# Two-layer sequence model on one Trainium2 core: the second layer's TensorE instructions in a written order, with value matmuls by group and the last output split by heads

## The chip, the cores and the metric

The kernel runs on one core of one Trainium2 chip. The metric is device time in microseconds (us) of one execution. Everything is fp32. TensorE (PE) does all matrix products and all transposes, and writes to PSUM; VectorE (DVE), ScalarE (ACT) and GpSimd (POOL) do the rest; SyncE (SP) only issues transfers.

## The reference, cut to what matters

The input is 16 sequences of 256 tokens with 256 features. Both layers have the form x + s(xn) · silu(g(xn)), with xn the layer norm of x.

```
x  = L0_attn_x                               # [16, 256, 256]
xn = layernorm(x)
s  = linear recurrence(xn)                   # 32 complex states, scan over the 256 tokens
g  = silu(proj2(gelu(proj1(xn))))            # 256 -> 1024 -> 256
x  = x + s * g

xn = layernorm(x)
# s: latent attention, 16 heads, causal
q        = xn @ Wq                           # per head 128 'nope' + 64 'rope' features
kv       = xn @ Wkv_a                        # 64 latent + 64 rope features, one for all heads
c_kv     = rmsnorm(kv[:64]) * kv_norm_w
k_nope, v = split(c_kv @ Wkv_b)              # per head
scores   = (q_nope k_nope + rope(q_rope) rope(k_rope)) / sqrt(192), causal mask
s        = softmax(scores) @ v, all heads, @ Wo
# g: base linear + 2 of 8 low-rank experts, chosen by a router
g = silu(xn @ base_w.T + base_b + 2 * sum_e gate_e * (xn @ A_e) @ B_e)
x = x + s * g
```

## The kernel before, in words

The 4096 tokens are worked on in 8 chunks of 512 tokens (two sequences each); `X[ch]` stays in SBUF from beginning to end. Layer 0 runs over all chunks first, then layer 1.

**Layer 0** calls TensorE through a small wrapper, `pe = InOrder(nc.tensor)` (line 52 in the profile). It ties every TensorE instruction to the one before it, so that TensorE's program has them in the order in which the source calls them. Layer 0 also folds the key and value up-projections into the query and output weights (`wlat`, `wout`), so that attention in layer 1 works on the 64 latent features alone.

**Layer 1** calls `nc.tensor` itself. There the source order is a priority only, and a scheduler of the framework, working when the kernel is built, sets the order of each engine's instructions. The instructions of each engine then run in that fixed order, and wait for each other by semaphores.

The pieces of a chunk, with their lines:

- `norm_chunk`, `transpose_chunk` (`tp`, L160; copies into `xnT` L164 on ScalarE, L166 on VectorE),
- `kv_chunk` (`pkv`, L516): latent keys and values, the `row` tile, with a small chain over ScalarE, VectorE and GpSimd; `key_chunk` (`pk`, L546) transposes `row` into `kT`,
- `router_chunk` (`pm`, L560) with a long chain of small VectorE instructions for the two best experts, `mid_chunk` (`pmT`, L615), and `gate_part` 0 and 1 (`pg`, L628 and L632), after the second of which ScalarE applies Silu to the whole chunk (L635). Silu lies in another table of ScalarE than Exp, so that there is a table load before and one after it,
- `query_tile(ch, g, t)` (`pq`, L684): four tiles for a group `g` of four heads. Tiles 0 and 1 hold rope features; VectorE multiplies (L688), GpSimd adds (L700, L701) into `qrot`, and eight transfers on SP's queue bring the result into `qg`. Tiles 2 and 3 go to `qg` through ScalarE (L694),
- `finish_part(ch, j)` (`po`, L791): the output projection of 128 tokens, 8 matmuls over the pairs of heads, the product with the gate on VectorE (L796), the sum with `X` on GpSimd (L797), and a transfer to HBM issued by SP.

The attention is cut into **units**: a unit is one group of four heads of one sequence, so a chunk has 8 units and the kernel 64. The main loop has a step for each unit. In step `i` there are three `score_pack`s of unit `i` (`sc`, L726: mask L738 and maximum L740 on VectorE, Exp with its sum L745 on ScalarE, reciprocal L750 on VectorE, normalization of `pr` L753 on GpSimd), the three `turn_part`s of unit `i - 2` (`pt`, L765: four transposes into one PSUM bank and a copy into `pT` on ScalarE, L766), the `values` of the unit turned in the step before (`av`, L775, with a copy into `attT` L785), two query tiles of the next group, and at most two chunk pieces: one of the next chunk and one `finish_part` of the chunk before. In the source a step is:

```
for z in range(3):
    if u:
        score_pack(u, z)
    if v and z == 0:
        values(v)
    if w:
        turn_part(w, 2 - z)
    if z < 2:
        if nq:
            query_tile(nq[0], nq[1], nq[2] + z)
        if extra[z]:
            extra[z]()
```

PSUM has eight banks: pool `ps_m1` has four, which all the chunk pieces, `pq`, `av` and `po` take in turn; `ps_sc` has three, one for each pack of scores; `ps_pt` has one for the transposes. After the loop come the four `finish_part`s of the last chunk.

Of the kernel before, what the change touches and what calls it, by code (L numbers as in the profile page):

```python
# [18 lines left out]
P = 128  # L19
B, S, D = 16, 256, 256  # L20
NTOK = B * S
CH = 512
# [18 lines left out]
def tile_two_layers(ctx: ExitStack, tc: tile.TileContext, d: dict, out: bass.AP):  # L41
# [114 lines left out]
    def transpose_rows(psum, ptag, src, dst, tag, layer=0):  # L156
        for c in range(2):
            ps = psum.tile([P, CH], F32, tag=ptag, name=f"tp_{tag}_{c}")
            for j in range(TPC):
                (pe if layer == 0 else nc.tensor).transpose(  # L160
                    ps[:, j * P : (j + 1) * P], src[:, j, c * P : (c + 1) * P], ident
                )
# [319 lines left out]
    sm = ctx.enter_context(tc.tile_pool(name="sm1", bufs=3))  # L482
    x1 = ctx.enter_context(tc.tile_pool(name="x1", bufs=2))
    qm = ctx.enter_context(tc.tile_pool(name="qm1", bufs=3))
    qr = ctx.enter_context(tc.tile_pool(name="qr1", bufs=2))
# [19 lines left out]
    def transpose_chunk(ch):  # L505
        k = chunks[ch]
        k.xnT = x1.tile([P, 2, CH], F32, tag="xnT", name=f"xnT1_{ch}")
        transpose_rows(ps_m1, "m1", k.xn, k.xnT, f"1_{ch}", layer=1)

    def kv_chunk(ch):  # L510
# [3 lines left out]
        for j in range(TPC):  # L514
            for c in range(2):
                nc.tensor.matmul(  # L516
# [4 lines left out]
        sq = a2.tile([P, TPC, KVL], F32, tag="sq", name=f"sq_{ch}", bufs=1)  # L521
# [10 lines left out]
        ra = a2.tile([P, TPC, ROPE], F32, tag="ra", name=f"ra_{ch}", bufs=1)  # L532
        rb = a2.tile([P, TPC, ROPE], F32, tag="rb", name=f"rb_{ch}", bufs=1)
# [7 lines left out]
    def key_chunk(ch):  # L541
# [3 lines left out]
        for j in range(TPC):  # L545
            nc.tensor.transpose(pk[:, j * P : (j + 1) * P], row[:, j, :], ident)  # L546
# [3 lines left out]
    def router_chunk(ch):  # L550
# [3 lines left out]
        mid = a2.tile([P, TPC, P], F32, tag="mid", name=f"mid_{ch}", bufs=1)  # L554
        for jp in range(2):
            pm = ps_m1.tile([P, 2, 256], F32, tag="m1", name=f"pm_{ch}_{jp}")
            for j2 in range(2):
                j = 2 * jp + j2
                for c in range(2):
                    nc.tensor.matmul(  # L560
# [40 lines left out]
        mg = a2.tile([P, TPC, P], F32, tag="mg", name=f"mg_{ch}", bufs=1)  # L601
        for j in range(TPC):
            nc.vector.tensor_tensor(
                mg[:, j, :].rearrange("p (e r) -> p e r", r=LR),
# [3 lines left out]
        k.mg = mg  # L608

    def mid_chunk(ch):  # L610
# [3 lines left out]
        for j in range(TPC):  # L614
            nc.tensor.transpose(pmT[:, j * P : (j + 1) * P], mg[:, j, :], ident)  # L615
        k.mT = a2.tile([P, CH], F32, tag="mT", name=f"mT_{ch}")
        nc.vector.tensor_copy(k.mT, pmT)

    def gate_part(ch, jp):
# [5 lines left out]
        for j2 in range(2):  # L625
            cols = slice((2 * jp + j2) * P, (2 * jp + j2 + 1) * P)
            for c in range(2):
                nc.tensor.matmul(  # L628
# [3 lines left out]
            nc.tensor.matmul(pg[:, j2, :], k.mT[:, cols], wlb, start=False, stop=True)  # L632
# [26 lines left out]

    class Group:  # L660
# [4 lines left out]
    def query_tile(ch, g, t):  # L665
# [12 lines left out]
        for c in range(2):  # L678
# [5 lines left out]
            nc.tensor.matmul(ps, w, k.xnT[:, c, :], start=(c == 0), stop=(c == 1))  # L684
# [24 lines left out]
    class Unit:  # L709


        def __init__(self, i):
# [5 lines left out]
            self.nm = sm.tile([P, NQ], F32, tag="nm", name=f"nm_{self.n}")  # L718
            self.sr = sm.tile([P, NQ], F32, tag="sr", name=f"sr_{self.n}")

    def score_pack(u, pi):
        k, b, pack = chunks[u.ch], u.b, PACK[pi]
        qg = groups[u.ch, u.g].qg
        sc = ps_sc.tile([P, CH], F32, tag="sc", name=f"sc_{u.n}_{pi}")
        for a, o in pack:
            nc.tensor.matmul(  # L726
# [31 lines left out]
    def turn_part(u, z):  # L758
        if z == 2:
            u.pT = pp.tile([P, 12, P], F32, tag="pT", name=f"pT_{u.n}")  # L760
        pt = ps_pt.tile([P, CH], F32, tag="pt", name=f"pt_{u.n}_{z}")
        for y in range(4):
            a, kb = BLOCKS[4 * z + y]
            o = OFF[a] + kb * P
            nc.tensor.transpose(pt[:, y * P : (y + 1) * P], u.pr[:, o : o + P], ident)  # L765
        nc.scalar.copy(u.pT[:, 4 * z : 4 * z + 4, :], pt.rearrange("p (y f) -> p y f", y=4))  # L766

    def values(u):
        k, b = chunks[u.ch], u.b
        av = ps_m1.tile([P, 2, S], F32, tag="m1", name=f"av_{u.n}")  # L770
        for p2 in range(2):
            for kb in range(2):
                for hh in range(2):
                    hc = slice(32 * (2 * p2 + hh), 32 * (2 * p2 + hh) + 32)
                    nc.tensor.matmul(  # L775
# [7 lines left out]
        if b == 0:  # L783
            k.attT.append(a2.tile([P, 2, CH], F32, tag="attT", name=f"attT_{u.n}", bufs=6))
        nc.vector.tensor_copy(k.attT[u.g][:, :, b * S : (b + 1) * S], av)  # L785

    def finish_part(ch, j):
        k = chunks[ch]
        po = ps_m1.tile([P, CH], F32, tag="m1", name=f"po_{ch}_{j}")
        for p in range(NPAIR):  # L790
            nc.tensor.matmul(  # L791
                po[:, 0:D], k.attT[p // 2][:, p % 2, j * P : (j + 1) * P], wout[:, p, :],
                start=(p == 0), stop=(p == NPAIR - 1),
            )
        o = a2.tile([P, D], F32, tag="o", name=f"o_{ch}_{j}")
# [3 lines left out]
        nc.sync.dma_start(out_dram[t0 : t0 + P, :], o)  # L799

    for k in chunks:
        k.attT = []
    norm_chunk(0)
    transpose_chunk(0)
    for t in range(4):
        query_tile(0, 0, t)
    kv_chunk(0)
    router_chunk(0)
    key_chunk(0)
    mid_chunk(0)  # L810
    for jp in range(2):
        gate_part(0, jp)
# [3 lines left out]
    LAG = 2  # L816
    LAST = NCH * PER
    units = {}
    turned = None
    for i in range(LAST + LAG + 1):  # L820
# [116 lines left out]
```

## Time and profile before

| what | value |
|---|---|
| time, median of 3 runs | 1108.28 us (1103.82 to 1109.83) |
| profiled execution: time | 1110.37 us |
| profiled execution: span of the trace | 1107.9 us |
| mean granted TensorE clock | 0.991 |
| busy: PE, PEld | 1032.7 us (93%), 743.7 us (67%) |
| busy: DVE, ACT, POOL | 523.9, 506.3, 401.9 us (47%, 46%, 36%) |
| layer 1's first TensorE instruction | at 289.38 us |
| first score matmul | at 318.09 us |
| last score matmul | starts at 1069.8 us |

The page gives the busy time of each engine, its costliest groups of instructions by source line, and the chain that ended last. PE is the matmul part of TensorE and PEld its weight load; every fp32 matmul stands twice among the records, so that "x16" in the timeline are eight matmuls of the source. In the timeline a line is a run of equal instructions: start, length, engine, source line, tile written and tiles read, and in brackets the idle time of the engine just before it with what ended that. The ends of matmuls are modelled and overlap a little with the next start, so that the step from start to start is the better measure.

### The profile page before, as it was taken

What the parts mean: (1) busy time and instruction counts of PE and PEld (TensorE: products, weight loads), DVE (VectorE), ACT (ScalarE), POOL (GpSimd) and SP (SyncE); (2) the same over time, 40 slices, a digit from 0 to 9 for tenths busy, and PEclk for the clock granted to TensorE, in tenths of its full rate; (3) what the DMA queues carried; (4) which work ended last, traced back from release to release, by engine and by line L of the source; (5) the groups of instructions that cost most, each with busy time, mean ns of one, the idle gap of its engine ahead of it and who ended that gap; (6) DMA issues with size and microseconds to landing.
All of it is one profiled execution on the core that took longest, in us unless ns stands there. A gap on an engine that the chain in (4) does not pass through costs nothing.

```text
span 1107.9 us, 16585 instructions
## 1 busy us (share of the span) xinstructions
PE 1032.7 (93%) x5442; PEld 743.7 (67%) x5442; DVE 523.9 (47%) x1841; ACT 506.3 (46%) x1520; POOL 401.9 (36%) x718
## 2 busy tenths in 40 slices
PE   5899999999889989999999999899999989999987
PEld 2666677666666667776776677577667767776765
DVE  7731253221667555545544454464465445545331
ACT  2223222333245575454546445654555474455450
POOL 2243342222524434333344333343344334334431
PEclk9999999999989999999999999999999999999999
DMA  9430000000011121111111211111111211112110
GB/s 307 133 101 10 0 10 10 10 10 10 11 24 24 25 34 25 30 25 20 30 29 26 30 33 29 20 25 29 25 23 33 36 26 25 29 25 32 25 22 20
DMA packets 155462, 38.57 MB, mean 35 GB/s; under 512 B 137585, under 2 KB 153841, under 8 KB 155377
## 3 DMA queue, kind: packets, MB, share of 16 engines
q1 hardware_dynamic: 153680, 35.93, 15.9%
q10 hardware_dynamic: 1696, 1.58, 0.5%
q8 instruction: 44, 0.72, 0.3%
q14 instruction: 42, 0.34, 0.1%
HBM read 14.42 MB, written 4.19 MB: 17 GB/s over the span
## 4 chain that ended last, share of the span: by engine, by line
PE 80%; ACT 8%; DVE 6%; issue 3%; POOL 1%; DMA 1%; POOLq 0%; ACTq 0%; SPq 0%; DVEq 0%
PE pq L684 17%; PE sc L726 11%; PE pf L52 9%; PE po L791 9%; PE ph L52 9%; PE av L775 8%; PE pt L765 7%; ACT pr L745 3%; PE pg L628 3%; ACT qg L694 2%; ACT pT L766 2%; PE pg L632 1%; PE py L52 1%; PE pm L560 1%; PE pkv L516 1%
## 5 line engine op out<-in xcount | busy, mean ns | idle before, releaser
L753 POOL TENSOR_SCALAR pr<-pr,sr 128x256 f32<-128x256 f32 (+7 forms) x512 | 189.3, 389 | 291.5 <-DVE sr L750 220.9
L745 ACT ACTIVATE pr<-sc,nm 128x256 f32<-128x256 f32 (+7 forms) x512 | 189.0, 380 | 75.4 <-DVE nm L740 67.4
L766 ACT COPY pT<-pt 128x512 f32<-128x512 f32 x192 | 112.9, 588 | 240.6 <-PE pt L765 240.3
L726 PEld LDWEIGHTS sc<-kT,qg 128*128 128x128 f32 x1024 | 157.8, 191 | 37.5 <-issue 23.1
L726 PE MATMUL sc<-kT,qg 128*128 128x256 f32 (+7 forms) x1024 | 173.8, 303 | 3.7 <-ACT qg L694 2.9
L765 PE MATMUL pt<-ident,pr 128*128 128x128 f32 x768 | 123.8, 281 | 14.5 <-ACT pT L766 14.5
L740 DVE TENSOR_REDUCE nm<-sc 128x1 f32<-128x256 f32 (+7 forms) x512 | 127.8, 299 | 3.7
L775 PE MATMUL av<-pT,row 128*64 128x256 f32 (+1 forms) x1024 | 100.3, 338 | 27.2 <-ACT pT L766 27.2
L684 PE MATMUL pq<-xnT,wrope 128*128 128x512 f32 x256 | 121.6, 598 | 0.3 <-ACT xnT L164 0.3
L684 PE MATMUL pq<-xnT,wlat 128*128 128x512 f32 x256 | 120.7, 593 | 0.0
L791 PE MATMUL po<-wout,attT 128*128 128x256 f32 x512 | 115.9, 380 | 0.0
L791 PEld LDWEIGHTS po<-wout,attT 128*128 128x128 f32 x512 | 97.5, 191 | 25.0 <-issue 11.6
L52 PE MATMUL ph<-xnT,p1T 128*128 128x512 f32 x256 | 113.2, 600 | 0.0
L52 PE MATMUL pf<-p2T,hT 128*128 128x256 f32 x512 | 113.0, 379 | 0.0
L688 DVE TENSOR_TENSOR qmul<-pq,rot_q 128x512 f32<-128x512 f32 x128 | 84.1, 681 | 55.0 <-PE pq L684 55.0
L765 PEld LDWEIGHTS pt<-ident,pr 128*128 128x128 f32 x768 | 89.8, 147 | 29.0 <-issue 22.9
L775 PEld LDWEIGHTS av<-pT,row 128*64 128x64 f32 x1024 | 64.9, 139 | 62.4 <-ACT pT L766 40.8
L52 PEld LDWEIGHTS pf<-p2T,hT 128*128 128x128 f32 x512 | 96.7, 190 | 13.3 <-issue 0.5
L745 ACT ACTIVATION_READ_ACCUMULATOR pr<-sc,nm 128x1 f32 x512 | 103.9, 203 | 0.0
L52 PEld LDWEIGHTS ph<-xnT,p1T 128*128 128x128 f32 x256 | 49.1, 193 | 59.5 <-issue 58.1
L694 ACT ACTIVATE qg<-pq 64x512 f32<-64x512 f32 x128 | 75.8, 592 | 28.3 <-PE pq L684 26.4
L701 POOL TENSOR_TENSOR qrot<-qmul,qmul 128x512 f32<-128x512 f32 x32 | 40.7, 1273 | 88.2 <-DVE sr L750 53.9
(174 smaller groups left out, 1040.3 us busy)
## 6 DMA issues: line engine op xcount, KB each, us to landing
qg<-qrot SPq DMA_DIRECT2D x256, 64.0 KB, 2.2
out_dram<-o SPq DMA_DIRECT2D x32, 128.0 KB, 1.7
x<-in_x_dram SPq DMA_DIRECT2D x7, 512.0 KB, 8.7
wqn<-in_wq_nopeT_dram SPq DMA_DIRECT2D x4, 512.0 KB, 4.5
wo<-in_Wo_dram SPq DMA_DIRECT2D x4, 512.0 KB, 5.6
w<-v SPq DMA_DIRECT2D x16, 128.0 KB, 2.3
wraw<-in_wq_rope_dram SPq DMA_DIRECT2D x1, 1024.0 KB, 9.8
x<-in_x_dram SPq DMA_DIRECT2D x4, 128.0 KB, 3.4
```

Of the source, the lines that this page charges most:

```text
L52: r = getattr(self.engine, name)(*args, **kw)
L684: nc.tensor.matmul(ps, w, k.xnT[:, c, :], start=(c == 0), stop=(c == 1))
L688: nc.vector.tensor_tensor(q.mul[t][:, r, :].rearrange("p (b s) -> p b s", b=2), ps2, bc(rot_q[:, r, :], 2), ALU.mult,)
L694: nc.scalar.mul(q.qg[0:64, :, 2 * (t - 2) + hh, :], ps[64 * hh : 64 * hh + 64, :].rearrange("p (a q) -> p a q", q=32), SCALE,)
L726: nc.tensor.matmul(sc[:, o : o + 32 * (a + 1)], qg[:, b * NQ + a, :, :].rearrange("p h q -> p (h q)"), k.kT[:, b * S : b * S + 32 * (a + 1 ...
L740: nc.vector.tensor_reduce(u.nm[:, a : a + 1], sc[:, o : o + 32 * (a + 1)], AX.X, ALU.max, negate=True)
L745: nc.scalar.activation(u.pr[:, OFF[a] : OFF[a] + w], sc[:, o : o + w], AF.Exp, bias=u.nm[:, a : a + 1], accum_out=u.sr[:, a : a + 1],)
L753: nc.gpsimd.tensor_scalar(v, v, u.sr[:, a : a + 1], 1.0, ALU.mult, ALU.mult)
L765: nc.tensor.transpose(pt[:, y * P : (y + 1) * P], u.pr[:, o : o + P], ident)
L766: nc.scalar.copy(u.pT[:, 4 * z : 4 * z + 4, :], pt.rearrange("p (y f) -> p y f", y=4))
L775: nc.tensor.matmul(av[64 * hh : 64 * hh + 64, p2, P * kb : S].rearrange("p (a q) -> p a q", q=32), k.row[:, 2 * b + kb, 0:KVL], u.pT[:, 8: ...
L791: nc.tensor.matmul(po[:, 0:D], k.attT[p // 2][:, p % 2, j * P : (j + 1) * P], wout[:, p, :], start=(p == 0), stop=(p == NPAIR - 1),)
```

## The change

1. **Written order.** All TensorE calls of layer 1 go through `pe` as well, so that TensorE's program follows the source.
2. **Values by group.** `values` is called in odd steps only, for units `i - 5` and `i - 4` together, just after the first score pack. `pT` gets three buffers (two before).
3. **Chunk pieces dealt anew.** Silu's half `gate_part(ch, 1)` moves to step 1 of its own chunk, the router from step 3 to 5, `kv_chunk` from 2 to 3, key and mid together to step 6, `gate_part(ch + 1, 0)` to 7. `finish_part`s stay in steps 3 to 6. In even steps with one piece it goes into the second slot.
4. **Start.** `kv_chunk(0)` comes first after the transposes, the last two query tiles after the router and the keys; `mid_chunk(0)` and the gate halves move into steps 0 and 1 of the loop.
5. **End.** The last chunk's output is split by heads: the matmuls over the first 6 pairs of heads of all four row blocks run after the last transposes and before the last two `values`, in four PSUM banks (three of them from `ps_sc`), and those of the last 2 pairs after.
6. **Output transfers** are issued by GpSimd instead of SP.
7. **Buffers.** Small tiles 3 to 2, `qmul` 3 to 2, `qrot` 2 to 1, `mT` 2 to 1; `sq`, `ra`, `rb`, `mid` share one tile, and `mg` is written over `mid`.

```diff
-                nc.tensor.matmul(                      # and so in every piece of layer 1
+                pe.matmul(
...
-    sm = ctx.enter_context(tc.tile_pool(name="sm1", bufs=3))
+    sm = ctx.enter_context(tc.tile_pool(name="sm1", bufs=2))
...
-    qm = ctx.enter_context(tc.tile_pool(name="qm1", bufs=3))
-    qr = ctx.enter_context(tc.tile_pool(name="qr1", bufs=2))
+    qm = ctx.enter_context(tc.tile_pool(name="qm1", bufs=2))
+    qr = ctx.enter_context(tc.tile_pool(name="qr1", bufs=1))
...
-        sq = a2.tile([P, TPC, KVL], F32, tag="sq", name=f"sq_{ch}", bufs=1)
+        tmp = a2.tile([P, 3, TPC, KVL], F32, tag="tmp", name=f"tmp_{ch}", bufs=1)
+        sq, ra, rb = tmp[:, 0], tmp[:, 1], tmp[:, 2]
...
-            u.pT = pp.tile([P, 12, P], F32, tag="pT", name=f"pT_{u.n}")
+            u.pT = pp.tile([P, 12, P], F32, tag="pT", name=f"pT_{u.n}", bufs=3)
...
-    def finish_part(ch, j):
+    def finish_begin(ch, j, p0, p1):
         k = chunks[ch]
-        po = ps_m1.tile([P, CH], F32, tag="m1", name=f"po_{ch}_{j}")
-        for p in range(NPAIR):
-            nc.tensor.matmul(
-                po[:, 0:D], k.attT[p // 2][:, p % 2, j * P : (j + 1) * P], wout[:, p, :],
+        if p0 == 0:
+            pool, tag = (ps_sc, "sc") if ch == NCH - 1 and j < 3 else (ps_m1, "m1")
+            k.po[j] = pool.tile([P, CH], F32, tag=tag, name=f"po_{ch}_{j}")
+        for p in range(p0, p1):
+            pe.matmul(
+                k.po[j][:, 0:D], k.attT[p // 2][:, p % 2, j * P : (j + 1) * P], wout[:, p, :],
                 start=(p == 0), stop=(p == NPAIR - 1),
             )
+
+    def finish_part(ch, j, p0=0):
+        k = chunks[ch]
+        finish_begin(ch, j, p0, NPAIR)
+        po = k.po[j]
...
-        nc.sync.dma_start(out_dram[t0 : t0 + P, :], o)
+        nc.gpsimd.dma_start(out_dram[t0 : t0 + P, :], o)
...
     transpose_chunk(0)
-    for t in range(4):
+    kv_chunk(0)
+    for t in range(2):
         query_tile(0, 0, t)
-    kv_chunk(0)
     router_chunk(0)
     key_chunk(0)
-    mid_chunk(0)
-    for jp in range(2):
-        gate_part(0, jp)
+    for t in range(2, 4):
+        query_tile(0, 0, t)
...
+    FINISH = (3, 4, 5, 6)
+    units = [Unit(i) for i in range(LAST)]
+    for i in range(LAST + 4):
...
+        if i == 0:
+            extra.append(lambda: mid_chunk(0))
+        if i == 1:
+            extra.append(lambda: gate_part(0, 0))
+        if r == 1 and ch < NCH:
+            extra.append(lambda: gate_part(ch, 1))
+        if 0 < ch < NCH and r in FINISH:
+            extra.append(lambda: finish_part(ch - 1, FINISH.index(r)))
         if ch + 1 < NCH:
             extra += {
                 0: [lambda: norm_chunk(ch + 1)],
                 1: [lambda: transpose_chunk(ch + 1)],
-                2: [lambda: kv_chunk(ch + 1)],
-                3: [lambda: router_chunk(ch + 1)],
-                4: [lambda: key_chunk(ch + 1)],
-                5: [lambda: mid_chunk(ch + 1)],
-                6: [lambda: gate_part(ch + 1, 0)],
-                7: [lambda: gate_part(ch + 1, 1)],
+                2: [],
+                3: [lambda: kv_chunk(ch + 1)],
+                4: [],
+                5: [lambda: router_chunk(ch + 1)],
+                6: [lambda: key_chunk(ch + 1), lambda: mid_chunk(ch + 1)],
+                7: [lambda: gate_part(ch + 1, 0)],
             }[r]
...
+        if len(extra) == 1 and r % 2 == 0:
+            extra.insert(0, lambda: None)
+        if i == LAST + 2:
+            extra = [lambda: [finish_begin(NCH - 1, j, 0, 6) for j in range(TPC)]]
+        if i == LAST + 3:
+            extra = [lambda: None, lambda: [finish_part(NCH - 1, j, 6) for j in range(TPC)]]
         for z in range(3):
-            if u:
-                score_pack(u, z)
-            if v and z == 0:
-                values(v)
-            if w:
-                turn_part(w, 2 - z)
+            if i < LAST:
+                score_pack(units[i], z)
+            if z == 0 and i % 2 and i >= 5:
+                values(units[i - 5])
+                values(units[i - 4])
+            if 2 <= i < LAST + 2:
+                turn_part(units[i - 2], 2 - z)
...
+            for e in extra[:1] if z == 0 else extra[1:] if z == 1 else []:
+                e()
```

## The prediction, made before the changed kernel ran

> **What bounds the kernel now.** I read the busy row first, then the busy time by stage, then TensorE's waits inside the main loop, then the timeline around each kind of wait. The stages (columns: stretch, length, PE, PEld, DVE, ACT, POOL busy, granted clock, DMA share, GB/s):
>
> ```profile
> PE 1032.7 (93%) x5442; PEld 743.7 (67%) x5442; DVE 523.9 (47%) x1841; ACT 506.3 (46%) x1520; POOL 401.9 (36%) x718
> ...
> 0.00:290.00 290.00, 271.74 (x1032) 182.15 (x1033) 110.15 (x373) 83.07 (x111) 86.99 (x86) 1.00 0.19 58
> 290.00:330.00 40.00, 32.37 (x137) 22.49 (x136) 28.18 (x86) 15.48 (x38) 16.39 (x21) 0.87 0.12 19
> ...
> 318.10:1070.10 752.00, 713.22 (x4167) 526.26 (x4165) 389.18 (x1399) 408.40 (x1376) 297.45 (x608) 1.00 0.17 28
> 1070.10:1089.50 19.40, 12.84 (x102) 8.35 (x101) 3.50 (x13) 7.79 (x24) 4.07 (x12) 0.93 0.00 1
> ```
>
> TensorE is the bound: in the main loop (318.1 to 1070.1) it is busy 713.2 of 752.0 us, and no other engine is above 55%. So an order of work can win at most what TensorE waits: 38.8 us in the loop, some 8 us before it (318.1 minus 289.4 against 21 us of work), and some 7 us in the stretch after it. Who it waits for in the loop (us in total, times, longest):
>
> ```profile
> PE av L775 <- ACT pT L766: 25.1, 24, 2.1
> PE pt L765 <- ACT pT L766: 9.9, 7, 1.4
> PE sc L726 <- ACT qg L694: 2.9, 8, 0.4
> ```
>
> Nearly all of it is ScalarE's copy of transposed probabilities. The `av` waits have one cause: values are called a step after their last transposes, with only a score pack (0.8 us) between, while a copy takes 588 ns and stands behind Exp instructions in ScalarE's queue. The `pt` waits have another: Silu with its two table loads. In the timeline, TensorE first, then ScalarE:
>
> ```profile
> 592.62 0.75 PE L726 MATMUL sc<-kT,qg 128*128 128x96 f32 x6
> 594.79 0.63 PE L765 MATMUL pt<-ident,pr 128*128 128x128 f32 x4 [1.42 <-ACT pT L766]
> ...
> 590.58 1.06 ACT L635 ACTIVATE g<-g 128x1024 f32<-128x1024 f32 x1 [0.83 <-DVE g L633]
> 591.64 1.28 ACT L745 ACT_TABLE_LOAD   x1
> ...
> 594.06 0.59 ACT L766 COPY pT<-pt 128x512 f32<-128x512 f32 x1
> 594.52 1.21 ACT L694 ACTIVATE qg<-pq 64x512 f32<-64x512 f32 x2
> ```
>
> The pattern repeats: this wait stands at 695.28 and at 794.34, so a chunk takes 99.06 us, of which 0.67, 0.67, 1.42, 0.36 and 2.10 are waits. TensorE's own work is thus 93.8 us a chunk, which the change leaves as it is. Before the loop and after it:
>
> ```profile
> 304.63 0.66 PE L546 MATMUL pk<-ident,row 128*128 128x128 f32 x4 [3.13 <-POOL row L538]
> 309.49 1.09 PE L615 MATMUL pmT<-ident,mg 128*128 128x128 f32 x4 [4.20 <-DVE mg L603]
> 310.37 1.91 PE L628 MATMUL pg<-wbase,xnT 128*128 128x256 f32 x4
> ...
> 1071.51 0.66 PE L765 MATMUL pt<-ident,pr 128*128 128x128 f32 x4
> 1072.89 0.66 PE L765 MATMUL pt<-ident,pr 128*128 128x128 f32 x4 [0.73 <-ACT pT L766]
> ...
> 1089.48 14.48 PE L791 MATMUL po<-wout,attT 128*128 128x256 f32 x64
> ```
>
> Two waits of 7.3 us together, then half the clock for some 6 us (`pg` takes 1.91 where the same four take 1.03 from 315.49 on); at the end, three transposes at 1.4 us each because one PSUM bank is filled and emptied in turn, and all 32 `po` at last.
>
> **The change part by part.** The order of instructions of the built changed kernel can be read engine by engine; I use it for who stands ahead of whom, and the trace for durations (start to start: score packs 0.82, 0.82, 0.59; `pt` 0.44; `pq` 1.72; `av` 1.45; `po` 3.46; `pkv` 1.78; `pm` 1.85; a gate half 2.6; `tp` 0.88).
>
> *Values by group.* A value matmul now follows its last copy by a whole step or more. The 24 waits of 25.1 us go, and nothing replaces them at `av`. What is late next is the transposes: in an even step no `av` stands between the last `pt` of the step before and the first of this one, only a score pack. Before, a pure turn of bank and copy took 1.4 us from `pt` to `pt`; here 0.44 and 0.82 lie between, so at least 0.15 us is short. In the built order that copy stands ahead of the next three Exps, and behind the `qg` pair (1.2 us from the end of `pq`, against 1.03 us of TensorE work when no piece follows). I take 0.2 us in three of the four even steps of a chunk, and 0.5 us where `pq` is the last before (step 7 to 0, `qg` then holds up the scores too).
>
> *Silu.* It moves to step 1, before an even step. From the end of the gate half: VectorE's sum until 0.9, Silu until 1.9, table until 3.2, three Exps until 4.4, the copy of the middle `pt` until 5.0. TensorE has 4.45 us of work there (0.82 + 0.44 + 1.72 + 0.88 + 0.59), so the last `pt` waits 0.6. Then `qg` until 6.2 against 5.6: the scores wait 0.6. Then `xnT`, three Exps and the last copy until 8.2, against 7.0: the first `pt` of step 2 waits 1.2. Together 2.4 us, where before it was 1.42 + 0.36. This part loses.
>
> So a chunk has about 2.4 + 0.5 + 0.3 = 3.2 us of waits, against 5.2. For the eight chunks 26 us, against 38.8.
>
> *Pieces dealt anew.* The same instructions, each once. Moved past VectorE's and GpSimd's queues: the router's chain (8 us of VectorE's queue with the score work that it is mixed with) has 10.9 us of TensorE work until `pmT`; the chain of `row` has two steps until `pk`. In step 3 the `kv` chain makes VectorE wait for GpSimd's power (1.0 us) ahead of the next mask, behind which is the copy of the second `pt`; a `po` (3.46) follows it, so it is covered. If that cover were gone, it would cost some 2 us a chunk. *Fewer buffers*: each next writer comes two steps or more after the last reader (`qrot`: the 8 transfers on SP's queue land 2.2 us after issue; the next sum on GpSimd is two steps later). Nothing, with up to 1 us a chunk as the other end.
>
> *Start.* The loop begins earlier, with 5.6 us of work moved into it (`pmT` 0.43, gate halves 5.2). `pkv` ends at 292.5, `pq` 0 and 1 at 296.0, the first half of `pm` at 297. The second needs the bank of `pkv`: it is the fourth tile after it in a pool of four. That bank comes free when VectorE has done `xn` of the next chunk (it took 291.1 to 295.7), the sums and the rope products: some 3 us of its own work and GpSimd's power of 1.0, so 300.8. `row` follows at 301.6, `pk` until 303.5, the two `pq` until 307.8. The rope part needs GpSimd (2.5 us) and a landing (2.2 us) after 303: 308, then `qg` to 309.2. I take 310 for the first score, against 318.1.
>
> *TensorE's clock, trace against rule.* In the trace a wait of 4.20 us is followed by 6 us at half speed, and of the waits of 2.10 us one (616.23, where `av` took 2.83 instead of 1.52) and not that at 716.71. The Trainium skill (TensorE: Matmul & The Clock Gate, section "Why this matters for your kernels") says to have no idle gap over about 3 us between bursts. By the rule alone only the start is at risk (the wait for the bank is 3.8 us; 3 us are in the 310). By the trace the change also removes slowdowns after 2.10 us: the chunks from 394.56 to 494.10, 594.79 and 695.28 took 99.5, 100.7 and 100.5 instead of 99.06, 3.5 us more; 1.3 of it is that `av`, and I take 2 as won. By the rule it would be 0, and the sum 16 instead of 18.
>
> *End.* From the last score: the last `pt` of unit 61 waits in ScalarE behind three Exps until 2.7; three `pt` 1.4 us apart until 6.0; two `av` until 8.9; three `pt` until 12.2; 24 `po` of 0.43 until 22.6; two `av` until 25.5; 8 `po` until 29.0. With 1.3 us for a cold clock 30.3, against 33.8 (1070.1 to 1103.9). Two more `pt` pieces than before are done inside the loop (0.9 us there).
>
> *Output transfers from GpSimd.* 32 of 128 KB. The trace has no transfer from this queue. Nearest row: `out_dram<-o` from SP lands 1.7 us after issue and costs GpSimd nothing. The skill (DMA: Bandwidth & Descriptors, section "Anatomy of one DMA — SWDGE (gpsimd) path") has 2.0 us plus bytes over 436 KB/us, so 2.3 us, and a later section ("SWDGE vs HWDGE vs iDMA") has GpSimd's own cores write the descriptors: a rule against this change. In the loop GpSimd is busy 40%, and has a step until `pr` is turned, so up to 2 us each is hidden. At the end the four sums (0.72) come 0.86 us apart: at 1 us of GpSimd for an issue the last is 2.9 us late, at none it is on time, and the landing adds 0 to 0.6. Both ends: 0 and 3.5; I take 1.5, between them as no run decides.
>
> **The sum.** Loop: 713.2 + 5.6 + 0.9 + 26 = 745.7, from 310 to 1055.7: 14.4 earlier. End: 3.5 less, 1.5 more. Clock: 2. Together 18 us. The profiled execution took 1110.37 (span 1107.9, 2.5 around it), which would become 1092; it stands 2.1 above the median of the runs, 1108.28, which becomes **1090**.
>
> **Rivals.** Half a per cent, 5.5 us, is about what a measurement of this kernel can tell from no change.
>
> 1. *The waits nearly vanish (0.17).* If Silu's chain finds gaps that my count misses (ScalarE is at 54%), the loop keeps 8 us instead of 26: 1072. For it: half of the waits have one cause. Against: the table loads stand where I counted them in the built order.
> 2. *The gain is handed back (0.15).* The waits at `av` only move to `pt`, the loop keeps 38 us or a little more, and the end gains nothing: 1098 to 1110, about 1104. For it: one bank for `pt`, unchanged, and even steps without `av`. Against: 0.82 us of scores lies between.
> 3. *Slower by the single `pt` bank (0.11).* If the last copy of an odd step comes behind the Exps of its third score pack in each chunk, every even step waits like the 1.42 of the Silu place: 31 steps x 1.42 = 44, less the 4 counted: 1130. It decides from 0.76 us a step (18 + 5.5 over 31). For it: in-order TensorE can't step past the waiting transpose, and the scheduler before could. Against: in the built order this holds for the last step only. A range for this case is 1114 to 1131.
> 4. That the order is not what it says is excluded: the built program follows the source on TensorE.
>
> **How the numbers follow.** The likeliest, 0.57, is 1090, by itself 1082 to 1097 (waits 20 to 33, transfers 0 to 3.5, start 308 to 313). The range takes in the gain handed back and the waits gone: 1070 to 1106; above it lie rival 3 and a little of rival 2, and below it little. Faster by over 0.5% (under 1102.7): 0.57 + 0.17 + 0.07 of rival 2 = 0.81. Within: 0.08. Slower: 0.11.
>
> **What would show it.** In the profile after: no wait of `av` for `pT` in the loop; `pt` waits for `pT` up, mostly in step 2 of each chunk behind a table load, 2 us or so; a chunk of about 97 us from Silu to Silu; the first score near 310 with a wait for a bank or for `row` before it; the last `po` 30 us after the last score. I'm wrong if `pt` waits over 0.7 us in every even step, if the scores wait for `qg` in each group, or if GpSimd's transfers hold up `pr`.

## The result, and the profile after

| what | before | after |
|---|---|---|
| time, median of 4 runs | 1109.05 us (1103.82 to 1109.83) | 1093.01 us (1091.11 to 1095.63) |
| profiled execution: time, span | 1110.37, 1107.9 us | 1091.11, 1089.3 us |
| chunk, from one `pkv` to the next | 99.06 us | 95.36 us |
| TensorE busy, sum of its waits | 1032.7, 71.2 us | 1028.9, 51.6 us |

The ratio is 0.987, with a 95% interval of 0.983 to 0.990: 1.3% faster, and 3 us from the predicted 1090. The medians differ by 16.0 us, the two profiled spans by 18.6: the profiled execution after was the lowest of its four. (The sum of waits, here and below, adds all lines of the view of waits for TensorE; some 18 us of it lie in layer 0 in every kernel.)

The busy row of the page after, then the busy time by stage (stretch, length, PE, PEld, DVE, ACT, POOL busy, granted clock, DMA share, GB/s): the loop from first to last score, the tail to the last `po`, the rest.

```profile
PE 1028.9 (94%) x5442; PEld 742.3 (68%) x5442; DVE 524.8 (48%) x1841; ACT 506.9 (47%) x1520; POOL 420.3 (39%) x750
...
310.40:1050.10 739.70, 717.88 (x4200) 532.40 (x4200) 394.57 (x1416) 412.02 (x1380) 316.32 (x642) 0.99 0.16 28
1050.10:1080.50 30.40, 25.23 (x157) 19.77 (x156) 4.83 (x13) 6.22 (x20) 3.45 (x9) 0.94 0.00 1
1080.50:1089.30 8.80, 0.23 (x2) 0.00 (x0) 0.85 (x2) 0.00 (x0) 3.71 (x6) 0.82 0.17 61
```

The loop waits 21.8 us now (739.7 less 717.9), against 38.8. Who it waits for there (us in total, times, longest; the 3.7 us for the landing in `qg` end where the loop begins, and are not in the 21.8):

```profile
PE pt L52 <- ACT pT L767: 13.7, 16, 1.6
PE sc L52 <- ACT qg L694: 6.2, 18, 0.7
PE sc L52 <- DMA qg<-qrot: 3.7, 1, 3.7
PE pt L52 <- POOL pr L754: 1.9, 1, 1.9
```

The 25.1 us of `av` are gone to the last tenth. The transposes and the scores wait more than before (9.9 and 2.9 us then). The timeline shows the start of the loop (with SyncE's eight transfers into `qg`), the Silu place of one chunk, and the end on VectorE and GpSimd:

```profile
299.82 1.17 PE L52 MATMUL pm<-wmid,xnT 128*128 128x136 f32 x8 [3.46 <-DVE tmp L536]
...
302.25 5.87 SPq L704 DMA_DIRECT2D qg<-qrot  x8
...
310.44 1.08 PE L52 MATMUL sc<-kT,qg 128*128 128x256 f32 x4 [3.73 <-DMA qg<-qrot]
...
606.62 0.63 PE L52 MATMUL pt<-ident,pr 128*128 128x128 f32 x4 [0.54 <-ACT pT L767]
607.61 1.08 PE L52 MATMUL sc<-kT,qg 128*128 128x256 f32 x4 [0.36 <-ACT qg L694]
609.68 0.63 PE L52 MATMUL pt<-ident,pr 128*128 128x128 f32 x4 [0.99 <-ACT pT L767]
...
1079.76 0.59 POOL L807 DMA_DIRECT2D out_dram<-o  x1 [0.30 <-POOL o L805]
...
1081.90 0.42 DVE L804 TENSOR_TENSOR o<-po,g 128x256 f32<-128x256 f32 x1 [2.38 <-DMA out_dram<-o]
...
1085.06 0.56 POOL L807 DMA_DIRECT2D out_dram<-o  x1 [0.30 <-POOL o L805]
```

With 0.31 us before another score pack (585.92), a chunk waits 0.31 + 0.54 + 0.36 + 0.99 = 2.20 us, all in steps 0 to 2. Of the 18.6 us between the spans, 7.7 come from the earlier first score, 12.3 from the loop, 3.4 from the tail; 4.8 are given back after the last `po`.

### The profile page after: what moved, and what is told of

The parts are those of the page before. It is cut to its first block, busy times and chain, and to the rows that moved or that the text cites. A ratio compares the mean times of both kernels' runs of the same rounds, so it can differ in the third digit from the quotient of the medians.

```text
span 1089.3 us, 16537 instructions
## 1 busy us (share of the span) xinstructions
PE 1028.9 (94%) x5442; PEld 742.3 (68%) x5442; DVE 524.8 (48%) x1841; ACT 506.9 (47%) x1520; POOL 420.3 (39%) x750
## 4 chain that ended last, share of the span: by engine, by line
PE 81%; ACT 8%; DVE 6%; POOL 2%; DMA 1%; issue 1%; SPq 0%; ACTq 0%; POOLq 0%; DVEq 0%
PE pq L52 17%; PE sc L52 11%; PE po L52 10%; PE pf L52 9%; PE ph L52 9%; PE av L52 8%; PE pt L52 7%; PE pg L52 4%; ACT pr L746 3%; ACT qg L694 2%; PE py L52 1%; PE pm L52 1%; PE pkv L52 1%; PE pb L52 1%; DVE nm L741 1%; ACT L746 1%
## 5 line engine op out<-in xcount | busy, mean ns | idle before, releaser
L52 PE MATMUL pq<-xnT,wrope 128*128 128x512 f32 x256 | 125.6, 615 | 0.0
L52 PE MATMUL av<-pT,row 128*64 128x256 f32 (+1 forms) x1024 | 91.3, 331 | 0.0
L751 DVE RECIPROCAL sr<-sr 128x3 f32<-128x3 f32 (+1 forms) x192 | 32.3, 168 | 82.0 <-ACT pr L746 74.7
```

What stands on the lines that cost most here:

```text
L52: r = getattr(self.engine, name)(*args, **kw)
L751: nc.vector.reciprocal(u.sr[:, lo:hi], u.sr[:, lo:hi])
```

## The experiments

The change is three things at once: an order (written in the source, or set by the scheduler), a lag (how many steps the values stand behind their scores), and a dealing of the pieces with start and end. The theory after the result was that of the prediction: the lag takes the `av` waits away and the written order costs little. The rival: the order itself pays or costs. Unless said otherwise a kernel differs from its base by the diff shown alone; times are medians, ratios are to the kernel before on the same chip (1109.55 or 1109.65 us).

### 1. The written order alone

Base: before.

```diff
-                nc.tensor.matmul(        # and in every piece of layer 1
+                pe.matmul(
```

> The kernel before with one edit: all TensorE calls of layer 1 go through the in-order wrapper; steps, lags, pieces, start, end, transfers and buffers as before. Theory A (the gain comes from where the source puts the values and pieces, and the written order is only the means to have it so): values still stand one score pack behind the last copy of their transposes, so TensorE waits some 0.5 us for ScalarE's copy in each of 64 steps, in place of the 25 us before; start and end as before. About 1107 us, between 1100 and 1118. Theory B (the written order itself is the gain, because the scheduler's order is poor): near the changed kernel, 1093 to 1098.

Measured: 1112.42 us, ratio 1.0035 (1.002 to 1.005). A fits. Inside the loop `av` waits less (14.1 instead of 25.1 us), scores more:

```profile
PE av L52 <- ACT pT L766: 14.1, 17, 1.4
PE pt L52 <- ACT pT L766: 10.1, 8, 1.4
PE sc L52 <- ACT qg L694: 7.5, 17, 0.7
```

So the order alone wins nothing. Beside the old lag it costs little, 2.9 us.

### 2. The changed kernel, order left to the scheduler

Base: after.

```diff
-                pe.matmul(               # and in every piece of layer 1
+                nc.tensor.matmul(
```

> The changed kernel with one edit: the TensorE calls of layer 1 go to the engine directly, so that the framework's scheduler sets their order, with the new lag, pieces, start, end, transfers and buffers. Theory A (the lag and the dealing are the gain): no wait of the value matmuls for the copies, 1091 to 1099 us. Theory B (the written order is the gain): waits of 25 us or more in the loop come back, 1104 to 1112.

Measured: 1057.16 us, ratio 0.953 (0.949 to 0.957): 36 us **faster** than the changed kernel. Both theories missed. All that TensorE waits for in the loop is one line:

```profile
PE sc L727 <- ACT pr L746: 0.8, 1, 0.8
```

At the place of the Silu, where the written order waits three times, the scheduler has put the next query tiles earlier, and cut one of them (six records of `pq`, one tile and a half, then the rest):

```profile
591.88 0.75 PE L727 MATMUL sc<-kT,qg 128*128 128x96 f32 x6
592.47 2.82 PE L684 MATMUL pq<-xnT,wrope 128*128 128x512 f32 x6
595.12 0.60 PE L766 MATMUL pt<-ident,pr 128*128 128x128 f32 x4
595.56 1.79 PE L727 MATMUL sc<-kT,qg 128*128 128x256 f32 x10
597.19 0.60 PE L766 MATMUL pt<-ident,pr 128*128 128x128 f32 x4
```

An order fixed for TensorE also changes what the scheduler makes of the other engines' orders, so that one of these could be the cause. The traces speak against it: in the chunk from 628.19 (here from 612.84) ScalarE has 1 of 112 instructions at another place, VectorE 10 of 181 and GpSimd none of 82.

New theory: the lag is worth far more than its 25 us, and the written order spends most of it by standing still before scores and transposes while a query tile behind them could run.

### 3. Outputs issued by SyncE

Base: after.

```diff
-        nc.gpsimd.dma_start(out_dram[t0 : t0 + P, :], o)
+        nc.sync.dma_start(out_dram[t0 : t0 + P, :], o)
```

> The changed kernel with the output transfers issued by SP again. Theory A (GpSimd's transfers cost only at the end, where each of four issues lies in GpSimd's queue ahead of the next sum, and where the third product waits for the first landing as there are two output buffers): the stretch from the last output matmul to the end shrinks from 8.8 us to about 5, the rest stays: 1089 us, 1087 to 1091. Theory B (they also hold up the normalization of the probabilities in the loop): the loop from first to last score, 739.7 us, shrinks by 3 us or more as well, 1083 to 1086. Theory C (the end is long for another reason): 1093.

Measured: 1089.14 us, ratio 0.982 (0.979 to 0.985), 3.9 below after and in A's range. The loop's waits for ScalarE stay (13.7 us at `pt`, 6.3 at `sc`), so B falls. At the end VectorE's third product still waits for a landing, now from SyncE:

```profile
1082.83 0.42 DVE L804 TENSOR_TENSOR o<-po,g 128x256 f32<-128x256 f32 x1 [1.81 <-DMA out_dram<-o]
```

There are two `o` buffers, so the third product needs the first transfer landed (1.7 us after issue in the median here, 2.0 from GpSimd). In the kernel before, the `po` came 3.5 us apart, and this wait didn't show.

### 4. The Silu half one step later

Base: after.

```diff
-        if r == 1 and ch < NCH:
+        if r == 2 and ch < NCH:
```

> The changed kernel with the second gate half, and so Silu with its two table loads, one step later: in the second slot of the even step 2 of its chunk, so that the step after it is an odd one with 2.9 us of value matmuls. Theory A (the waits of 0.54, 0.36 and 0.99 us a chunk behind Silu come from the even step with no value matmuls to cover ScalarE's chain): they vanish, 1.9 us in each of eight chunks less some new waits of 0.3, so the loop shrinks by 10 to 15 us: 1080 us, 1077 to 1085. Theory B (Silu's chain on ScalarE costs the same wherever it stands): 1091 to 1095.

Measured: 1085.38 us, ratio 0.979 (0.976 to 0.983): 7.6 us better, in A's direction, short of its 8 to 16. A chunk takes 94.57 us (722.97 to 817.54) and waits 0.31, 0.60 and 0.51. The start of the loop got worse: a transposes' wait of 3.9 us that the changed kernel hasn't. Silu's place counts, but in the steady chunk it brings only 0.8 us.

### 5. A query tile ahead, order still written

Base: after.

```diff
+        early = nq and i % 2 == 0
         for z in range(3):
+            if early and z == 0:
+                query_tile(nq[0], nq[1], nq[2])
             if i < LAST:
                 score_pack(units[i], z)
...
-                if nq:
+                if nq and not (early and z == 0):
```

> The changed kernel, its order still written out; in each even step the first of the two query tiles is called ahead of the step's first scores and no longer after its first transposes. Nothing else. In the changed kernel a chunk's waits of TensorE are 0.31 and 0.36 us (scores on qg), 0.54 and 0.99 us (transposes on pT); three of the four stand in even steps just behind the new place of the tile. Theory A (a written order costs only where work that could run stands behind work that waits; the scheduler gains by calling a query tile there): 0.31, 0.36 and 0.99 us go, 1.66 us in each of 7 chunks, with some 3 us of the first chunk and half of the 3.73 us wait of the first score: 1074 to 1082 us, chunk about 93.7 us. Rival B (ScalarE is late by itself after the Silu; a moved tile only moves the wait to the next transposes of the step): 1088 to 1094 us, with waits of the same sum at other places.

Measured: 1067.4 us, ratio 0.962 (0.959 to 0.965). B falls; A's mechanism holds, and 25.6 us is more than its 11 to 19. The chunk is 93.17 us, and one wait is left in it (compare the three of the changed kernel above):

```profile
684.34 0.63 PE L52 MATMUL pt<-ident,pr 128*128 128x128 f32 x4 [0.54 <-ACT pT L767]
684.80 1.88 PE L52 MATMUL pq<-xnT,wrope 128*128 128x512 f32 x4
686.52 0.97 PE L52 MATMUL sc<-kT,qg 128*128 128x256 f32 x4
687.40 0.63 PE L52 MATMUL pt<-ident,pr 128*128 128x128 f32 x4
```

Why more: the waits fell from 51.6 to 33.6 us, 18.0, and TensorE's busy time from 1028.9 to 1020.6, 8.3. A steady chunk gives 2.2 us; from the first score to the third `pkv` it takes 114.4 us in place of 127.0, so that 12.6 us of the gain lie there, where some 3 were expected. One part of the busy time: after waits close together matmuls took up to twice their time for some microseconds. In the changed kernel, step 2 of the last chunk:

```profile
988.04 0.62 PE L52 MATMUL pt<-ident,pr 128*128 128x128 f32 x4 [1.41 <-ACT pT L767]
989.03 1.08 PE L52 MATMUL sc<-kT,qg 128*128 128x256 f32 x4 [0.36 <-ACT qg L694]
990.61 1.08 PE L52 MATMUL pt<-ident,pr 128*128 128x128 f32 x4 [0.51 <-ACT pT L767]
991.49 3.12 PE L52 MATMUL pq<-xnT,wrope 128*128 128x512 f32 x4
```

The same four `pq` take 1.88 us at 684.80. The kernel with the tile ahead has no such slow `pq` inside its loop. How the 8.3 us divide was not worked out further.

### 6. The lag alone

Base: before, scheduler. Old dealing, start and end.

```diff
-    qr = ctx.enter_context(tc.tile_pool(name="qr1", bufs=2))
+    qr = ctx.enter_context(tc.tile_pool(name="qr1", bufs=1))
...
-        row = a2.tile([P, TPC, P], F32, tag="row", name=f"row_{ch}")
+        row = a2.tile([P, TPC, P], F32, tag="row", name=f"row_{ch}", bufs=3)
...
-            u.pT = pp.tile([P, 12, P], F32, tag="pT", name=f"pT_{u.n}")
+            u.pT = pp.tile([P, 12, P], F32, tag="pT", name=f"pT_{u.n}", bufs=3)
...
-            if v and z == 0:
-                values(v)
+            if z == 0 and i % 2 and i >= 5:
+                values(units[i - 5])
+                values(units[i - 4])
```

> The kernel before, TensorE still ordered by the scheduler, old dealing, old start and old end; only the values are called in pairs, five and four units behind the scores (three pT buffers; a third buffer of row and one qr buffer less for the room). In the kernel before, the values waited 27.2 us in sum for the copies of pT. Theory A (the lag is the larger half of what the dealt kernel with the scheduler gained, 52 us): these 27.2 us go, with some 2 to 4 us that half-clock matmuls after them cost, and the transposes' 14.5 us stay: 1076 to 1086 us. Rival B (the copies are late as a whole, so that the wait passes to the next transposes; the gain came from the dealing): 1098 to 1110 us, transposes waiting 30 us or more.

Measured: 1055.42 us, ratio 0.952 (0.949 to 0.955): 54 us, twice what A gave it, and as much as experiment 2. The view of waits is empty inside its loop. One chunk (columns as above), in which TensorE is busy all of the time:

```profile
687.84:780.89 93.05, 93.05 (x554) 69.88 (x553) 50.31 (x182) 53.12 (x176) 38.28 (x79) 1.00 0.17 30
```

The transposes' waits went too, against A: there the scheduler again splits a query tile around scores and transposes.

```profile
615.33 0.63 PE L765 MATMUL pt<-ident,pr 128*128 128x128 f32 x4
615.80 1.02 PE L684 MATMUL pq<-xnT,wrope 128*128 128x512 f32 x2
616.66 0.97 PE L726 MATMUL sc<-kT,qg 128*128 128x256 f32 x4
617.47 0.60 PE L765 MATMUL pt<-ident,pr 128*128 128x128 f32 x4
617.91 1.02 PE L684 MATMUL pq<-xnT,wrope 128*128 128x512 f32 x2
```

### 7. The dealing without the lag

Base: experiment 2.

```diff
-            if z == 0 and i % 2 and i >= 5:
-                values(units[i - 5])
-                values(units[i - 4])
+            if z == 0 and 3 <= i < LAST + 3:
+                values(units[i - 3])
```

> The changed kernel with its layer-1 matmuls left to the scheduler (1057 us as measured) and the values called as before, one unit in each step, three units behind its scores. Dealing of the chunk pieces, start and end as changed. Theory A (the lag is worth about 27 us): values wait again for pT, 15 to 30 us in sum: 1073 to 1088 us. Rival B (the dealing alone gives the copies of pT their time): 1056 to 1063 us and no value wait above 5 us in sum.

Measured: 1092.97 us, ratio 0.986 (0.982 to 0.989): 36 us slower than with the lag, 5 above A's range, and B falls. Its loop waits again (total, times, longest):

```profile
PE av L776 <- ACT pT L767: 16.8, 23, 1.8
PE pt L766 <- ACT pT L767: 7.7, 9, 2.3
PE sc L727 <- ACT qg L694: 3.1, 9, 0.4
```

### 8. The best of these: scheduler, SyncE, four `o` buffers

Base: experiment 2.

```diff
-        o = a2.tile([P, D], F32, tag="o", name=f"o_{ch}_{j}")
+        o = a2.tile([P, D], F32, tag="o", name=f"o_{ch}_{j}", bufs=4)
...
-        nc.gpsimd.dma_start(out_dram[t0 : t0 + P, :], o)
+        nc.sync.dma_start(out_dram[t0 : t0 + P, :], o)
```

> The changed kernel with its layer-1 matmuls left to the scheduler (1057 us as measured), the output transfers issued by SyncE in place of GpSimd, and four o buffers in place of two. From the last matmul's end to the span's end that kernel takes 9.1 us, with a wait of 2.39 us of the third output product for the landing of the first transfer. Theory A (GpSimd's issues and the two buffers are what made the end 8.8 to 9.1 us long against 4.0 before): the stretch is 4.5 to 6 us: 1052 to 1055 us. Rival B (four transfers one after the other land no sooner, whoever issues them): 1056 to 1058 us.

Measured: 1051.97 us, ratio 0.949 (0.946 to 0.951), at the edge of A. It beats both kernels, the changed one by 41 us. From its last `po` to the end it takes 4.0 us, and no product waits for a landing: its four products stand 0.9 us apart.

```profile
1044.06 0.42 DVE L804 TENSOR_TENSOR o<-po,g 128x256 f32<-128x256 f32 x1 [0.36 <-PE po L794]
...
1044.92 0.42 DVE L804 TENSOR_TENSOR o<-po,g 128x256 f32<-128x256 f32 x1 [0.44 <-PE po L794]
...
1045.37 2.92 SPq L807 DMA_DIRECT2D out_dram<-o  x4
```

### 9. The lag in written order, old dealing

Base: experiment 6.

```diff
-                nc.tensor.matmul(        # and in every piece of layer 1
+                pe.matmul(
```

> The lag-only kernel (1055 us with the scheduler) with all layer-1 calls of TensorE in written order; old dealing, old start, old end. It fills the empty corner between written order alone (1112 us), the lag alone (1055 us) and both with the dealt pieces (1093 us). Theory A (the written order costs some 36 us beside the lag too, as the same kind of step stands before a late copy): 1078 to 1096 us, transposes waiting 14 us or more. Rival B (it is the dealing that makes the written order costly; the old pieces after each scores pack are long enough): 1056 to 1064 us.

Measured: 1097.41 us, ratio 0.990 (0.987 to 0.992): 42 us slower than the same source left to the scheduler, 1.4 above A. B falls: with the lag the written order is dear in both dealings. Why it costs 42 us here and 3 beside the old lag was not separated. What it waits for most in the loop:

```profile
PE pt L52 <- ACT pT L766: 16.1, 18, 1.5
PE sc L52 <- ACT qg L694: 7.1, 17, 0.6
```

### 10. Two banks for the transposes

Base: after.

```diff
-    ps_m1 = ctx.enter_context(tc.tile_pool(name="ps_m1", bufs=4, space=PSUM))
-    ps_pt = ctx.enter_context(tc.tile_pool(name="ps_pt", bufs=1, space=PSUM))
+    ps_m1 = ctx.enter_context(tc.tile_pool(name="ps_m1", bufs=3, space=PSUM))
+    ps_pt = ctx.enter_context(tc.tile_pool(name="ps_pt", bufs=2, space=PSUM))
```

> The changed kernel, written order, with two PSUM buffers for the transposed probabilities in place of one, and three for all other layer-1 products in place of four. Theory A (the transposes wait because their one buffer is read by the copy in front of them; with two the 0.54 and 0.99 us of a chunk go, the scores' 0.31 and 0.36 stay): 16.8 us of transposes' waits and some 4 us of half clock less: 1072 to 1082 us. Rival B (three other buffers are too few: the query, value and output matmuls wait for them): 1090 to 1110 us, with new waits of pq, av or po.

Measured: 1071.5 us, ratio 0.966 (0.964 to 0.968), 21.5 below after: A, half a microsecond better than its range. No `pt` waits in the loop, and three banks are enough for the rest; the scores' wait grows, 1.06 us in step 2 of each chunk:

```profile
PE sc L52 <- ACT qg L694: 11.7, 17, 1.9
PE sc L52 <- DVE sc L739: 2.7, 1, 2.7
PE sc L52 <- DMA qg<-qrot: 1.8, 1, 1.8
```

### 11. The written order mended in three places

Base: experiment 5; SyncE and four `o` buffers as in experiment 8.

```diff
-            if early and z == 0:
+            if early and z == 0 and r != 2:
...
                 values(units[i - 4])
+            if r == 1 and z == 2 and ch < NCH:
+                query_tile(*divmod(nxt + 1, NG), 0)
...
+        if LAST <= i < LAST + 2:
+            extra = [
+                lambda: finish_begin(NCH - 1, 2 * (i - LAST), 0, 4),
+                lambda: finish_begin(NCH - 1, 2 * (i - LAST) + 1, 0, 4),
+            ]
         if i == LAST + 2:
-            extra = [lambda: [finish_begin(NCH - 1, j, 0, 6) for j in range(TPC)]]
+            extra = [lambda: [finish_begin(NCH - 1, j, 4, 6) for j in range(TPC)]]
```

> The kernel with the query tile ahead (1067 us, written order), and three edits more: in step 2 of a chunk that tile stands one place earlier still, ahead of the transposes that wait 0.54 us behind the Silu; the first four heads of the last chunk's output products stand between the last transposes (waits 0.18, 2.00, 0.73, 0.77, 0.73, 0.77 us); the outputs are issued by SyncE, with four o buffers. Theory A (a written order has no price of its own, only that of its places): 0.54 x 7 = 3.8, about 4.5 of the tail's 5.2 with 2 of half clock, and 4 to 5 at the end: 1051 to 1056 us, level with the scheduler. Rival B (an order without the scheduler's knowledge of times leaves other waits as these go): 1059 to 1066 us.

Measured: 1066.54 us, ratio 0.962 (0.959 to 0.964). A missed, and B's range by 0.5 us. The end is mended (4.0 us from the last `po`, and four of the tail's six waits gone), but the tile one place earlier made the loop worse: in step 2 0.55 us stays and 1.37 comes, and a chunk takes 94.61 us (712.89 to 807.50) against 93.17.

```profile
694.51 0.63 PE L52 MATMUL pt<-ident,pr 128*128 128x128 f32 x4 [0.55 <-ACT pT L767]
...
697.32 0.66 PE L52 MATMUL pt<-ident,pr 128*128 128x128 f32 x4 [1.37 <-ACT pT L767]
```

So B's sentence, that other waits appear as these go, holds for this try. The loop of experiment 5 with this end was not run, nor with the two banks of experiment 10, and whether a written order can come level with the scheduler stays open: none of these does.

### 12. Four steps of lag, no pairs

Base: experiment 6.

```diff
-            if z == 0 and i % 2 and i >= 5:
-                values(units[i - 5])
-                values(units[i - 4])
+            if z == 0 and 4 <= i < LAST + 4:
+                values(units[i - 4])
```

> The lag-only kernel (1055 us, scheduler) with the values not in pairs: one unit in every step, four units behind its scores. Before it is one unit in every step, three behind (1109.65 us). Theory A (the distance is what counts: with one step more every copy of pT is done): 1056 to 1066 us. Rival B (the pairing counts: 64 matmuls in one piece, and steps without values leave ScalarE its time): 1080 to 1105 us, the values or the transposes waiting 15 us or more.

Measured: 1066.11 us, ratio 0.961 (0.959 to 0.963), at the edge of A: the distance of one step more brings 43 of the 54 us. The pairs, with a fifth step for half of the units, bring the other 10.7, mostly not by waits (28.3 and 25.3 us in sum) but by work: TensorE is busy 1031.6 us without them and 1021.9 with them. One chunk without pairs:

```profile
695.13:789.63 94.50, 94.28 (x554) 69.77 (x552) 50.63 (x181) 52.75 (x176) 37.98 (x78) 1.00 0.17 29
```

A pair's `av` takes 2.82 us and a single one 1.52; from start to start, which the modelled ends don't touch, it is 2.75 and 1.45. So a pair saves 0.15 to 0.22 us, at most 0.9 of the 1.2 us of busy time a chunk. Where the rest lies, and why, was not separated: in experiment 6 the scheduler keeps 22 of the 32 pairs in one piece, and without pairs 52 of the 64 units.

### The three parts side by side

| values | dealing, start, end | scheduler | written order |
|---|---|---|---|
| three behind, single | old | 1109.6 | 1112.4 |
| three behind, single | new | 1093.0 | not run |
| five and four behind, paired | old | 1055.4 | 1097.4 |
| five and four behind, paired | new | 1057.2 | 1093.0 |

The difference of each profiled span to that of before is its difference in TensorE's waits, plus that in its busy time, plus what the end after the last `po` adds (4.8 us where there are two `o` buffers and GpSimd). This tells where the time lies, not why:

| kernel | waits | busy | end | sum | span |
|---|---|---|---|---|---|
| after | -19.6 | -3.8 | +4.8 | -18.6 | -18.6 |
| 5, tile ahead | -37.6 | -12.1 | +4.8 | -44.9 | -45.1 |
| 6, lag alone | -45.9 | -10.8 | 0 | -56.7 | -56.6 |
| 10, two banks | -29.5 | -12.7 | +4.8 | -37.4 | -37.6 |

## Why the prediction was right, point by point

The number was right, and so was the mechanism of its likeliest case: the waits of `av` go and part of them comes back at `pt` behind the Silu. That the span came out within 0.6 us (1089.3 for 1107.9 less 18) is luck, for the loop took 4.0 us less than counted and the end 3.3 more. And it did not see that the change holds a gain of 54 us and a cost of 36.

- **Values by group: right in kind, the gain too small.** The 25.1 us of `av` went, as written. The sum stopped there; experiment 6 shows that the lag with its pairs takes every wait out of the loop and 10.8 us of busy time with it. The step that failed is "TensorE's own work is thus 93.8 us a chunk, which the change leaves as it is": in experiments 6 and 12 the pairs are worth 1.2 us of it, and a chunk of the changed kernel has 93.2 us of work (95.36 less 2.20).
- **The transposes that are late next: right.** 2.20 us of waits a chunk against 3.2 in the sum: the places before the scores of step 0 and in the Silu steps are those named (0.6 + 0.6 + 1.2 there, measured 0.54 + 0.36 + 0.99). The 0.2 us in other even steps didn't come; the working names three such steps, which is 0.6 us, or 0.4 without the one behind the Silu, and its sum took 0.3.
- **The written order: its price is in those waits, but was not set against the scheduler.** Rival 3 had the reason: TensorE stands at a transpose that waits, and the scheduler, when the kernel is built, can put other work ahead of it. It was put at 0.11 and sized for the single bank alone. That bank costs 21.5 us (experiment 10), the place of the query tile 25.6 (experiment 5); the two overlap, since the scheduler's order (experiment 2), with one bank, waits only 0.8 us in its loop.
- **Start: the time right, the waits not.** First score at 310.4 for 310. The wait for the bank of `pkv` came at 3.46 us, but the first score waited 3.73 for the landing in `qg`, where the working leaves some 1.4 from the end of `pq` to the end of `qg`. It counted one landing of 2.2 us behind GpSimd's sums. SyncE took 5.87 us to issue the eight transfers, to 308.1, and the median landing of 2.3 us after that is 310.4. The sums began at 300.95 and not at 303, and so the two errors cancel. After the wait four `pq` took 3.58 us, for 1.88 at speed.
- **Loop: 739.7 us for 743.7** (745.7 less 2 of clock). It waits 21.8 us where the sum had 26, and is busy 717.9 where it had 719.7. The steady chunks wait less than counted, the first more, 5.6 us: 0.91, 1.63, 0.23, 1.90, 0.66 and 0.31.
- **Clock: trace over rule, but no gain.** The prediction took 2 us as won. It read one slow stretch after a wait of 2.10 us; the trace of before has a second, at 515.54 (shown in the last section). Slow stretches after waits of 1.9 us and less did come (`pt` at 352.27 takes 1.08 after 1.90), so the gap of about 3 us that the Trainium skill names (TensorE: Matmul & The Clock Gate, section "Why this matters for your kernels") is too wide here, as the trace of before had said. But the changed kernel still has them, its mean granted clock is no higher (0.989, and 0.991 before), and the `pq` on `wrope` grew from 121.6 to 125.6 us busy: the 2 us were not won.
- **End: 30.4 us for 30.3.** Its transposes come 1.4 us apart, as counted.
- **Output transfers: the term mis-sized most.** 4.8 us for 1.5, outside its bounds of 0 to 3.5. (Its "2.9 us late" at 1 us an issue is 2.6 by its own figures: three times 1.72 less 0.86.) At the end an issue holds GpSimd 0.56 to 0.59 us, within what was assumed, and a transfer lands after 2.0 us in the median, for the prediction's estimate of 2.3. Left out was that two `o` buffers make the third product wait for the first landing, since the `po` are now 0.86 us apart: 2.38 us, and the fourth product waits 1.20 more. Experiments 3 and 8 show the size: 3.9 us by SyncE on the changed kernel, where 1.81 us of that wait stay; 5.2 by SyncE with four buffers on experiment 2. Four buffers with GpSimd were not run. The Trainium skill (DMA: Bandwidth & Descriptors, section "SWDGE vs HWDGE vs iDMA") has GpSimd's cores compute the descriptors of such a transfer and gives plain transfers to SyncE or ScalarE; that rule has the right sign here, by the 3.9 us.
- **Rivals.** "The waits nearly vanish" (1072, at 0.17) is what experiments 2 and 6 do with the scheduler's order; in written order experiments 5 and 10 come near its number. "The gain is handed back" is true in part: of the 25.1 us of `av`, 3.8 came back at `pt` and 3.3 at `sc` with ScalarE as cause.

## What to carry to other kernels

Where an in-order engine waits for a copy, try first to move the reader one step further from it, and leave the order as it was: here one step was worth 43 us and with the pairs 54, and fixing the order as well took 42 of it back. When an order is written by hand, read every wait left in the steady loop and ask which piece behind the waiting one has its inputs already; one such call moved (experiment 5) was worth more than the whole change. And when pieces at the end are moved closer together, count the buffers of the last output: products 3.5 us apart hid a landing of 1.7 us, and at 0.86 us apart they did not.

## What the runs showed of the hardware

- Three waits of 1.41, 0.36 and 0.51 us within 4 us were followed by four `pq` in 3.12 us, where 1.88 is usual. Waits of 0.54, 0.36 and 1.00 us were followed by a slow stretch once (`pt` of 1.09 us at 417.45) and by none at 514.32, 609.68, 705.03, 800.39 and 895.75: the lengths of the waits alone don't decide it. In the kernel before, a wait of 2.10 us is followed by one here, and by none at 716.71:

```profile
515.54 1.56 PE L775 MATMUL av<-pT,row 128*64 128x256 f32 x16 [2.10 <-ACT pT L766]
517.03 1.11 PE L765 MATMUL pt<-ident,pr 128*128 128x128 f32 x4
517.93 3.06 PE L684 MATMUL pq<-xnT,wrope 128*128 128x512 f32 x4
```

- A 128 KB transfer issued by GpSimd lands 2.0 us after issue in the median and holds GpSimd 0.56 to 0.78 us (0.59 in the median); GpSimd stands idle 0.30 us between its own sum and the issue. Issued by SyncE it lands after 1.7 us.
- SyncE takes 5.87 us to issue eight transfers of 64 KB.
- The `av` of two units in one piece take 2.75 us from start to start, of one unit 1.45 us: two single pieces take 0.15 us more.
